# A sum over all rows of h: from VectorE (in layernorm and beside the products of q) to GpSimd, behind each store

## The chip, the cores and the metric

The kernel runs on one core of one Trainium2 chip. The metric is the device time of one execution in microseconds (us). Five engines work side by side and wait for each other by semaphores: TensorE (PE in the profile), VectorE (DVE), ScalarE (ACT), GpSimd (POOL) and SyncE (SP). DMA transfers are issued by SP, ACT and POOL from their own instruction streams; an issue that must wait holds up what is behind it in that stream.

## The reference

x is 2708 × 1024 (f32), adj is 2708 × 2708 with an entry of 1 with probability 0.0014771 (four per row on average), the weights are 1024 × 1024.

```python
h = relu(layernorm(x))
q = h @ W_q.T + b_q;  k = h @ W_k.T + b_k;  v = h @ W_v.T + b_v
z = (q @ k.T) / sqrt(1024)
z = z * adj;  z = where(z == 0, -10000, z)
out = softmax(z, axis=1) @ v
return x + relu(out)
```

For a row with neighbours the masked entries weigh nothing, so only the neighbours' rows are needed. A row without any neighbour has equal weights on all 2708 rows: for it the kernel needs the sum of all rows of h. That sum is what the change is about.

## The kernel before, in words

**The arithmetic.** Scores are h·M·hᵀ with M = W_qᵀ·W_k, formed once on TensorE (`part_of_m`, L348). "q" of a row is then h·M plus a bias row, its score with a neighbour is a dot product with that neighbour's row of h, and the output of a row is (the weighted sum of its neighbours' rows of h) times W_vᵀ. The 2708 rows make 22 tiles of 128 rows (tile 21 has 20).

**Stage 1, layernorm, edges and M** (until about 200 us). `follow` (L235) carries out strings of steps written by hand: `s` = `stats` (L188: load rows of x on SP, VectorE's mean and variance), `r` = `root` (L209: seven small operations, the last is r at L221), `a` = `apply` (L224), `e` = `edges` (L250: load a tile of adj on SP, ACT counts its entries at L256, VectorE finds their places by FIND_INDEX8 at L259 and sorts them into keys). In `apply`, ACT writes relu(layernorm) over the row tile (L230), POOL stores it to h_dram (L231), and, for tiles below EARLY = 9, VectorE adds it to hsum (L233), a 128 × 1024 tile whose column sums are the sum over all rows. Row tiles of x rotate over seven buffers and four more of the tag "q"; adj rotates over three. ACT's order is the written one in this stage, so an eviction of PSUM behind an L230 waits for it. VectorE's, SyncE's and POOL's order is set by a scheduler. Tiles 0 to 4 of q are formed here the plain way (`query`, L309), in natural order of rows.

**The sort.** Rows are sorted by their number of neighbours (`sort`, L467): VectorE makes `hot` (L484) after the last tile's edges, TensorE multiplies it (ps_in at L488, placed within tile 4's product), VectorE works out every row's place (pos_i at L502) and POOL writes the table (`put`, L445). From then on POOL gathers rows of h by the table (L425, L428).

**Stage 2, units.** The units are 8 pairs of tiles of q (5..20; unit numbers n = 0..7), then 10 pairs of output tiles (n = 8..17). Each is a Strassen-like product of seven blocks (`multiply`, L790): TensorE's block products at L780, `blocks` (L513) makes the operands (transposes at L274, sums on VectorE at L524), `q_results` (L821) and `o_results` (L851) take the results (q at L834, p at L859). Up to FIRST = 2 the rows of a pair come in natural order or by `first_rows`; from unit 2 on rows in the sorted order are gathered one unit and more ahead (`load_rows`).

**Attention** is one stream of VectorE steps in tile order 6,5,4,3,0,2,1,9,…: `scores` (L658; L664, 1.22 us a step, on the gathered row g and the query row pq), `weights` (L683; exp on ACT at L680, u on ACT at L709 or, in the two tiles 8 and 20 that hold rows without neighbours, at L703 from hsum) and `sums` (L713; L717, 1.28 us a step). The queries pq come by a gather from q_dram (tiles below 9) or a load from q_late, both on POOL. After each of the seven products `advance(share)` issues attention worth `share` us; an output pair whose rows are not yet done makes it catch up (`advance(1.0)` until done). From unit FIRST on VectorE's order is the written one, so a step of attention stands in front of or behind a product's sums as written.

**hsum before the change.** Tiles below 9 are summed in `apply`. The other rows are added when they have been gathered in sorted order for the pairs of q from unit 2 on: `sum_rows` (L921) adds the two row tiles of the next pair behind its operands' sums (L924, 12 additions), and one gather and addition of the last 20 rows (h_rest) stands in unit 2. `all_rows` (L926) then sums over partitions on TensorE (ps_h) in unit 6, and ACT writes the result back into hsum.

Of the kernel before, what the change touches and what calls it, by code (L numbers as in the profile page):

```python
# [18 lines left out]
P = 128  # L19
# [4 lines left out]
SLOTS = 16  # L24
# [6 lines left out]
EARLY = 9  # L31
# [24 lines left out]
def tile_preln_masked_attention(  # L56
# [12 lines left out]
    nc = tc.nc  # L69
# [6 lines left out]
    FULL = N // P  # L76
    REST = N - FULL * P
# [14 lines left out]
    h_dram = dram.tile([N, D], FT, name="h_dram")  # L92
# [24 lines left out]
    hsum = const.tile([P, D], FT, name="hsum")  # L117
# [36 lines left out]
    t = 0  # L154
    while t < NT:
# [4 lines left out]
        t = e  # L160
# [24 lines left out]
    def row_tile(name):  # L185
        return work.tile([P, D], FT, tag="row", name=name, bufs=ROWS)
# [37 lines left out]
    def apply():  # L224

        group, xs, r = normed.pop(0)
        for i, t in enumerate(group):
            t0, n = tiles[t]
            xt = xs[i]
            nc.scalar.activation(xt[:n], xt[:n], AF.Relu, bias=r[:n, 4, i:i + 1], scale=r[:n, 3, i:i + 1])  # L230
            nc.gpsimd.dma_start(h_dram[t0:t0 + n, :], xt[:n])  # L231
            if t < EARLY:
                nc.vector.tensor_add(hsum[:n], hsum[:n], xt[:n])  # L233

    normed, adj_loads = [], []  # L235

# [56 lines left out]
    def query(hT, banks, name, first=False, between=(), mid=None):  # L293

        q = work.tile([P, D], FT, tag="q", name=f"q_{name}", bufs=4)
        order = [(h, c) for h in range(NH) for c in range(DC)]
        if first:

            order.sort(key=lambda hc: hc[1] >= DC // 2)
        def evict(h):  # L300
            if h < len(between):
                follow(between[h])
            nc.scalar.copy(q[:, h * NB:(h + 1) * NB], banks[h])

        for h, c in order:
            if mid is not None and (h, c) == (1, 3):
                evict(0)
                mid(mm)
            mm = nc.tensor.matmul(banks[h], hT[:, c, :], M[:, c // 4, h, c % 4, :], start=False,  # L309
                                  stop=(c == DC - 1), skip_group_check=True)  # L310
        for h in range(NH) if mid is None else (1,):
            evict(h)
        return q
# [111 lines left out]
    def gather(dst, src, t, w, n, skip=False):  # L425
        off = bass.IndirectOffsetOnAxis(ap=ptab.bitcast(U32)[:n, t, w:w + 1], axis=0)
        if skip:
            return nc.gpsimd.indirect_dma_start(out=dst, out_offset=None, in_=src, in_offset=off,  # L428
                                                bounds_check=N - 1, oob_is_err=False)
        return nc.gpsimd.indirect_dma_start(out=dst, out_offset=None, in_=src, in_offset=off)  # L430

    rows_of = {}
    FIRST = (EARLY - SINGLE) // 2
# [77 lines left out]
    behind = []  # L511

    def blocks(xa, xb):  # L513


        ops = {}

        def held(name, bank):
            ops[name] = small(name).rearrange("p (c q) -> p c q", q=P)
            nc.scalar.copy(ops[name], bank)  # L520

        def put(name, a, b, op):
            ops[name] = small(name).rearrange("p (c q) -> p c q", q=P)
            behind.append(nc.vector.tensor_tensor(ops[name], a, b, op=op))  # L524

        def upper():
            held("a11", half_turned(xa, 0))
            held("a12", half_turned(xa, 1))

        def lower():  # L530
            held("a22", half_turned(xb, 1))
            a21 = half_turned(xb, 0)
            put("s1", ops["a22"], a21, ALU.add)
            put("s3", ops["a11"], a21, ALU.subtract)
            put("s2", ops["s1"], ops["a11"], ALU.subtract)
            put("s4", ops["a12"], ops["s2"], ALU.subtract)

        return ops, upper, lower
# [19 lines left out]
    for t in range(SINGLE):  # L558
# [7 lines left out]
        if t == SINGLE - 1:  # L566
# [3 lines left out]
        q = query(hT.pop(t), banks, f"e{t}", first=(t == 0), between=work_between[t] if t < 4 else (),  # L570
                  mid=sort_here if t == 4 else None)
# [197 lines left out]
    def advance(us):  # L769

        spent[0] -= us
        while spent[0] < 0:
            step = next(stream, None)
            if step is None:
                break
            spent[0] += step
# [5 lines left out]
    def banks_for(row):  # L782

        return_ = []
        for h in range(NH):
            return_.append(psum.tile([P, NB], FT, tag="acc", name=f"ps{h}"))
            nc.scalar.copy(return_[h], row[:, h * NB:(h + 1) * NB])
        return return_
# [91 lines left out]
    def send(keep=0):  # L880
        while len(sent) > keep:
            y, t = sent.pop(0)
            scatter(y, t, P)
# [8 lines left out]
    def of_wv(i, j):  # L892

        return wv[j][:, i * 4:(i + 1) * 4, :]
# [23 lines left out]
    last_q = len(q_pairs) - 1  # L918
    summed = []

    def sum_rows(rows, n=P):  # L921
        with tc.issue_after(behind[-1].ins):
            for row in rows:
                nc.vector.tensor_add(hsum[:n], hsum[:n], row[:n])  # L924

    def all_rows():  # L926

        for h in range(NH):
            ps_h = psum.tile([P, NB], FT, tag="tp", name="ps_h")
            nc.tensor.matmul(ps_h, ones, hsum[:, h * NB:(h + 1) * NB], start=True, stop=True)  # L930
            nc.scalar.copy(hsum[:, h * NB:(h + 1) * NB], ps_h)
        summed.append(True)

    for n, unit in enumerate(units):
        kind, ta, tb = unit
        now[0] = n
        if n == FIRST:
            ordered.enter_context(tc.manual_schedule(engines={mybir.EngineType.DVE}))
        if 1 <= n <= 3:

            i, j = ((0, 0), (1, 0), (1, 1))[n - 1]
            nc.sync.dma_start(m_dram[i, j], M[:, i, j])
        share = (19.0 if kind == "q" else 18.0) / 7
        nxt = units[n + 1] if n + 1 < len(units) else None
        results = (q_results if kind == "q" else o_results)(ta, tb)

        def after(i):
            if i in (2, 5):
                send()
            if n == FIRST - 1 and i == 2:  # L950

                chain.append(behind[-1])
                next(stream)
            if n == FIRST - 1 and i == 6:
                chain.append(behind[-1])
            if n >= FIRST or n == FIRST - 1 and i == 6:
                advance(share)
            if nxt is not None:

                if i == (3 if n == FIRST - 1 else 0):  # L960
                    ops_of[n + 1] = blocks(*rows_of[n + 1])
                    ops_of[n + 1][1]()
                if i == (5 if n == FIRST - 1 else 2):
                    ops_of[n + 1][2]()
                    rows = rows_of.pop(n + 1)
                    if nxt[0] == "q" and n + 1 >= FIRST:
                        sum_rows(rows)
                    if n == last_q - 1:
                        all_rows()
                if i == 3:  # L970
                    banks_of[n + 1] = banks_for(bp_sb)
                if i == 4 and n == FIRST:
                    rest = row_tile("h_rest")
                    gather(rest[:REST], h_dram[:, :], FULL, SLOTS, REST)
                    sum_rows([rest], REST)
                if i == 4 and n + 2 < len(units) and n + 2 not in rows_of:
                    while units[n + 2][0] == "o" and not done.issuperset(units[n + 2][1:]):
                        advance(1.0)
                    rows_of[n + 2] = load_rows(units[n + 2])
            if n == last_q - 1 and i == 4:  # L980

                nc.sync.dma_start(bp_sb, bv.to_broadcast([P, D]))
                nc.vector.tensor_sub(bp_sb[:, NB:], bp_sb[:, NB:], bp_sb[:, :NB])

            for k, at in enumerate(((0, 0), (0, 2), (0, 4), (0, 6), (1, 0), (1, 2), (1, 3))):
                if (n - last_q, i) == at:
                    place, src = ((M[:, 0, 0], of_wv(0, 0)), (T[:, 0], tv_dram[0]), (T[:, 1], tv_dram[1]),
                                  (M[:, 1, 0], of_wv(1, 0)), (T[:, 2], tv_dram[2]), (M[:, 1, 1], of_wv(1, 1)),
                                  (T[:, 3], tv_dram[3]))[k]
                    nc.sync.dma_start(place, src)  # L990

        multiply(ops_of.pop(n)[0], banks_of.pop(n), results, after, None)
# [46 lines left out]
    with tc.If(some > 0):  # L1039
        with tc.tile_pool(name="big", bufs=1, side="right") as big, tc.tile_pool(  # L1040
# [20 lines left out]
            with tc.For_i(0, NT) as i:  # L1061
                r0 = nc.snap(smin(i * P, N - P))
                rows = bass.ds(r0, P)
# [7 lines left out]
                q = gen.tile([P, D + 1], FT, tag="q", name="g_q")  # L1071
# [111 lines left out]
```

## Time and profile before

Three runs took 713.38, 713.4 and 713.5 us, median 713.4. The profile and the trace are of one execution of their own:

| what | value |
|---|---|
| profiled execution | 710.02 us, of which the span of the trace 708.2 |
| granted TensorE clock, mean | 0.995 |
| busy: PE, DVE, ACT, POOL | 676.4, 532.0, 252.1, 301.0 us |
| L233, hsum + x on VectorE | 9 additions, 10.8 us, 1.200 each |
| L924, hsum + qr on VectorE | 12 additions, 14.7 us, 1.227 each |
| L231, store of h on POOL | 22 issues, 0.536 each |
| L664 / L717, steps of attention | 94 of 1.223 / 79 of 1.282 |

A line of the profile gives the engine, the line of the kernel (L12), the operation, its output and inputs by the program's names, how often it ran, and what ended the idle time in front of it. A timeline's line begins with the start and the length in us from the start of the span; several instructions of one kind in succession are one line. The idle time of an engine that is not the bound costs nothing by itself.

### The profile page before, as it was taken

To read this page: it belongs to the slowest core of one execution; us is meant where nothing else is said; L and a number is where in the kernel's file an instruction comes from. 1 tells how busy PE (TensorE), PEld (TensorE's weight loads), DVE (VectorE), ACT (ScalarE), POOL (GpSimd) and SP (SyncE) were. 2 spreads that over 40 slices of the span, in tenths; PEclk is the share of its full clock that TensorE was granted. 3 is DMA by queue.
4 is the path that set the end of the run, shared out by engine and by line. 5 is a ranking of instruction groups with operands and counts; after the bars stand their busy time and mean duration, and the time that the engine had idled before them with its cause. 6 is when DMAs were issued, how large, how long until landed. Compare 5 with 4: busy or idle time off the path is not lost. (4 is left out here: it accounts for less than half of the span.)

```text
span 708.2 us, 6378 instructions
## 1 busy us (share of the span) xinstructions
PE 676.4 (96%) x1812; PEld 346.1 (49%) x1812; DVE 532.0 (75%) x1074; ACT 252.1 (36%) x378; POOL 301.0 (42%) x278
## 2 busy tenths in 40 slices
PE   6999999899999997998999999999999999799995
PEld 4776776444454452444444444444444444344442
DVE  6999848997992039899898898888999996851001
ACT  0077168768721221322322322232423423323220
POOL 2011010000256646867474462786567856231312
PEclk9999999999999999999999999999999999999999
DMA  9999699999996378877789899898789889473524
GB/s 346 406 408 336 269 321 401 409 344 385 393 362 214 121 279 287 296 264 254 266 266 363 313 412 377 238 324 244 226 244 283 271 255 264 118 208 102 138 41 135
DMA packets 62915, 198.02 MB, mean 280 GB/s; under 512 B 9910, under 2 KB 10262, under 8 KB 61468
## 3 DMA queue, kind: packets, MB, share of 16 engines
q0 software_dynamic: 34208, 107.76, 48.1%
q1 hardware_dynamic: 26652, 82.99, 30.8%
q10 hardware_dynamic: 2016, 6.82, 2.5%
q8 instruction: 16, 0.26, 0.1%
q14 instruction: 23, 0.19, 0.1%
HBM read 164.61 MB, written 46.51 MB: 298 GB/s over the span
## 5 line engine op out<-in xcount | busy, mean ns | idle before, releaser
L428 POOL DMA_INDIRECT g<-h_dram,tab x107 | 135.8, 1269 | 50.0 <-issue 22.6
L780 PE MATMUL psy<-T,s 128*128 128x512 f32 x288 | 129.6, 592 | 1.8 <-ACT u L804 1.8
L780 PE MATMUL ps<-M,a 128*128 128x512 f32 x288 | 130.3, 592 | 0.0
L664 DVE SCALAR_TENSOR_TENSOR junk<-g,pq 128x1024 uint8<-128x1024 f32 x94 | 114.9, 1223 | 17.8 <-DMA pq<-q_dram,tab 11.0
L355 PE MATMUL ps_m<-wk,wq 128*128 128x512 f32 x256 | 112.4, 601 | 5.5 <-DMA wq<-in_wq_dram 5.4
L717 DVE SCALAR_TENSOR_TENSOR u<-g,coef,u 128x1024 f32<-128x1024 f32 x79 | 101.3, 1282 | 9.4 <-ACT u L709 7.3
L355 PEld LDWEIGHTS ps_m<-wk,wq 128*128 128x128 f32 x256 | 80.1, 314 | 36.0 <-DMA wk<-in_wk_dram 5.4
L780 PEld LDWEIGHTS psy<-T,s 128*128 128x128 f32 x288 | 54.6, 190 | 70.6 <-issue 65.8
L780 PEld LDWEIGHTS ps<-M,a 128*128 128x128 f32 x288 | 53.4, 190 | 60.7 <-issue 60.5
L231 POOL DMA_DIRECT2D h_dram<-x x22 | 11.8, 536 | 166.9 <-ACT x L230 166.9
L259 DVE FIND_INDEX8 at<-ones,adj 128x8 uint32<-128x685 f32 (+1 forms) x88 | 75.3, 864 | 0.0
L780 PE MATMUL psy<-T,a 128*128 128x512 f32 x144 | 67.1, 610 | 8.4 <-DVE p L859 4.8
L309 PE MATMUL ps<-M,T_e 128*128 128x512 f32 x160 | 69.8, 593 | 1.8 <-ACT ps L290 1.8
L780 PE MATMUL ps<-T,s 128*128 128x512 f32 x144 | 65.4, 593 | 1.8 <-DVE s L524 1.8
L780 PE MATMUL ps<-M,s 128*128 128x512 f32 x144 | 65.2, 592 | 0.0
L256 ACT ACTIVATE sized<-adj 128x2708 uint8<-128x2708 f32 (+1 forms) x22 | 54.1, 2461 | 4.1 <-DMA adj<-in_adj_dram 4.0
L849 POOL DMA_INDIRECT y<-in_x_dram,tab x21 | 34.6, 1645 | 43.4 <-ACT y L864 20.7
L780 PEld LDWEIGHTS psy<-T,a 128*128 128x128 f32 x144 | 27.3, 194 | 44.8 <-issue 30.5
L309 PEld LDWEIGHTS ps<-M,T_e 128*128 128x128 f32 x160 | 30.0, 190 | 37.7 <-issue 35.2
L618 POOL DMA_INDIRECT out_dram<-y,tab x21 | 23.5, 1121 | 49.4 <-DMA y<-in_x_dram,tab 48.5
L780 PEld LDWEIGHTS ps<-M,s 128*128 128x128 f32 x144 | 27.3, 190 | 34.0 <-issue 34.0
L520 ACT COPY a<-pt 128x512 f32<-128x512 f32 x54 | 30.2, 592 | 32.2 <-PE pt L274 22.7
(197 smaller groups left out, 707.8 us busy)
## 6 DMA issues: line engine op xcount, KB each, us to landing
adj<-in_adj_dram SPq DMA_DIRECT2D x21, 1354.0 KB
x<-in_x_dram SPq DMA_DIRECT2D x21, 512.0 KB
h_dram<-x POOLq DMA_DIRECT2D x21, 512.0 KB
q_late<-q SPq DMA_DIRECT2D x12, 512.0 KB
pq<-q_late POOLq DMA_DIRECT2D x12, 512.0 KB
u_dram<-u POOLq DMA_DIRECT2D x9, 512.0 KB
or<-u_dram SPq DMA_DIRECT2D x9, 512.0 KB
wq<-in_wq_dram SPq DMA_DIRECT2D x8, 512.0 KB
```

The lines of the kernel that those rows point to most:

```text
L231: nc.gpsimd.dma_start(h_dram[t0:t0 + n, :], xt[:n])
L256: nc.scalar.activation(sized[:n], a[:n, :, :PW], AF.Abs, accum_out=total[:n, t:t + 1])
L259: nc.vector.max_index(at[:n, g, :], ones[:n, 0:8], a[:n, g, :])
L309: mm = nc.tensor.matmul(banks[h], hT[:, c, :], M[:, c // 4, h, c % 4, :], start=False, stop=(c == DC - 1), skip_group_check=True)
L355: nc.tensor.matmul(acc[i], lhs, wk_sb[o][:, cols], start=(o == 0), stop=(o == DC - 1))
L428: return nc.gpsimd.indirect_dma_start(out=dst, out_offset=None, in_=src, in_offset=off, bounds_check=N - 1, oob_is_err=False)
L520: nc.scalar.copy(ops[name], bank)
L618: to = nc.gpsimd.indirect_dma_start(out=out, out_offset=bass.IndirectOffsetOnAxis(ap=ptab.bitcast(U32)[:n, t, SLOTS:SLOTS + 1], axis=0), i ...
L664: chained(lambda: nc.vector.scalar_tensor_tensor(junk, g_of[t][s], 1.0, tq[t], op0=ALU.mult, op1=ALU.mult, accum_out=zall[:, t, s:s + 1]))
L717: chained(lambda: nc.vector.scalar_tensor_tensor(u, g_of[t][s], coef[:, at[t][s]:at[t][s] + 1], u, op0=ALU.mult, op1=ALU.add))
L780: nc.tensor.matmul(bank, a[:, c, :], b[:, c, :], start=False, stop=(c == 3), skip_group_check=True)
L849: nc.gpsimd.indirect_dma_start(out=y[:n], out_offset=None, in_=x, in_offset=off, compute_op=ALU.add)
```

## The change

Three things are changed. Every tile's addition to hsum in `apply`, for all 22 tiles, is made by GpSimd, on the same queue as the store of that tile and right behind it. The additions of gathered rows in the pairs of q, and the gather and addition of the last 20 rows, are left out. The share of attention issued per pair of products is 20 in the pairs of q and 19 in those of o, in place of 19 and 18.

```diff
@@ apply()
             nc.scalar.activation(xt[:n], xt[:n], AF.Relu, bias=r[:n, 4, i:i + 1], scale=r[:n, 3, i:i + 1])
             nc.gpsimd.dma_start(h_dram[t0:t0 + n, :], xt[:n])
-            if t < EARLY:
-                nc.vector.tensor_add(hsum[:n], hsum[:n], xt[:n])
+            nc.gpsimd.tensor_add(hsum[:n], hsum[:n], xt[:n])
@@ the units
-    def sum_rows(rows, n=P):
-        with tc.issue_after(behind[-1].ins):
-            for row in rows:
-                nc.vector.tensor_add(hsum[:n], hsum[:n], row[:n])
...
-        share = (19.0 if kind == "q" else 18.0) / 7
+        share = (20.0 if kind == "q" else 19.0) / 7
...
                     ops_of[n + 1][2]()
-                    rows = rows_of.pop(n + 1)
-                    if nxt[0] == "q" and n + 1 >= FIRST:
-                        sum_rows(rows)
+                    rows_of.pop(n + 1)
                     if n == last_q - 1:
                         all_rows()
...
-                if i == 4 and n == FIRST:
-                    rest = row_tile("h_rest")
-                    gather(rest[:REST], h_dram[:, :], FULL, SLOTS, REST)
-                    sum_rows([rest], REST)
```

The order of instructions changes with it where the scheduler decides. On POOL each of the 22 additions stands directly behind its store. On SP the load of x's tile 13 stands behind that of tile 11, those of tiles 16 and 17 behind four more loads of adj, the load of h_e7 behind adj 17 to 19 and that of h_e8 behind adj 20 and 21.

## The prediction

> **What bounds the kernel now.** I read the busy shares first, then TensorE's own idle gaps, then what the engines named in those gaps had waited for. Part 1 of the page, and a table by stretch (start and end, length, busy time with instruction count of PE, PEld, DVE, ACT, POOL, then granted clock, DMA share, GB/s):
>
> ```profile
> PE 676.4 (96%) x1812; PEld 346.1 (49%) x1812; DVE 532.0 (75%) x1074; ACT 252.1 (36%) x378; POOL 301.0 (42%) x278
> 100.00:130.00 30.00, 27.11 (x75) 18.50 (x75) 25.51 (x90) 20.93 (x30) 2.14 (x4) 1.00 1.02 390
> 130.00:200.00 70.00, 70.00 (x190) 32.83 (x189) 62.27 (x187) 47.85 (x56) 6.02 (x9) 1.00 1.00 378
> 264.00:325.00 61.00, 53.78 (x143) 24.77 (x142) 55.62 (x88) 14.83 (x26) 43.45 (x36) 0.97 0.84 287
> 325.00:485.00 160.00, 159.79 (x449) 75.83 (x449) 143.00 (x198) 45.45 (x81) 93.08 (x76) 1.00 0.88 309
> 485.00:618.00 133.00, 125.52 (x344) 58.41 (x343) 120.44 (x207) 46.12 (x83) 82.23 (x69) 1.00 0.80 240
> ```
>
> TensorE is the bound. In 130–200 and 325–485 it has no gap, though VectorE is 89% busy in both. So time is to be had only where PE idles: 2.9 us in 100–130, 7.2 in 264–325, 7.5 in 485–618, besides start and end. PE's timeline at those gaps (start, length, idle before it and its releaser in brackets), then ACT's and DVE's:
>
> ```profile
> 112.20 1.09 PE L274 MATMUL pt<-ident,h_e 128*128 128x128 f32 x8 [1.11 <-issue]
> 126.38 4.99 PE L309 MATMUL ps<-M,T_e 128*128 128x512 f32 x11 [1.78 <-ACT ps L290]
> 269.91 3.70 PE L780 MATMUL psy<-T,s 128*128 128x512 f32 x8 [1.83 <-ACT u L804]
> 283.83 5.40 PE L780 MATMUL psy<-T,a 128*128 128x512 f32 x8 [3.35 <-DVE q L834]
> 323.91 1.06 PE L274 MATMUL pt<-ident,qr 128*128 128x128 f32 x8 [2.04 <-DMA qr<-h_dram,tab]
> 611.40 3.70 PE L780 MATMUL psy<-T,a 128*128 128x512 f32 x8 [3.36 <-DVE p L859]
> ```
>
> ```profile
> 106.81 2.37 ACT L230 ACTIVATE x<-x,r 128x1024 f32<-128x1024 f32 x2 [6.29 <-DVE r L221]
> 121.53 2.37 ACT L230 ACTIVATE x<-x,r 128x1024 f32<-128x1024 f32 x2 [1.39 <-DVE r L221]
> ```
>
> ```profile
> 192.95 0.64 DVE L484 TENSOR_TENSOR hot<-deg,down 128x162 f32<-128x162 f32 x2
> 265.38 1.23 DVE L664 SCALAR_TENSOR_TENSOR junk<-g,pq 128x1024 uint8<-128x1024 f32 x1 [10.96 <-DMA pq<-q_dram,tab]
> 278.32 2.51 DVE L924 TENSOR_TENSOR hsum<-hsum,qr 128x1024 f32<-128x1024 f32 x2
> 602.84 1.23 DVE L664 SCALAR_TENSOR_TENSOR junk<-g,pq 128x1024 uint8<-128x1024 f32 x1 [4.80 <-DMA pq<-q_late]
> ```
>
> At 112 and 126 ACT's evictions stand in its written order behind layernorm's L230, which waited for VectorE's r. At 270, 284 and 611 VectorE is late, twice after it had itself waited for a transfer (10.96, 4.80). At 324 a gathered row is late. The product behind the 3.35 gap took 5.40 instead of about 3.6 (granted clock 0.72 in 284–290): 1.8 more lost there.
>
> **The change part by part.** The sum is made against the profiled execution, 710.02 us (span 708.2 and 1.8 around it), 3.4 below the median of 713.4; the difference in us is carried to the median.
>
> *Off VectorE.* Nine L233 adds, 10.8 us by the group's row (1.200 each); twelve L924 adds, 14.7 (1.227 each); one h_rest add, 1.2, with its gather on POOL (the add waited 1.7 for it). Together 26.7 us, but on an engine that costs time only at the gaps. All nine L233 adds lie before about 110; the others in the pairs of q from unit 2 on.
>
> *On to GpSimd.* Twenty-two adds, each right behind its store's issue (L231, 0.536 us), so 21 full and one of 20 rows. No row shows a GpSimd add. Low end: VectorE's own 1.20. High end: three passes of what a GpSimd memset of this size takes (L118, 0.942), 2.8. I take 1.9, two such passes, since two operands must be read: about 41 us, between 26 and 61. POOL is busy 8.2 of the 100 us from 100 to 200, so its time is covered by its own idleness. Behind each add stand the next stores of its group: the last of four comes up to 3 × (0.54 + 1.9 − 1.19) = 3.8 us later, 1.19 being ACT's pace (2.37 for two). Behind the last adds stand the three memsets (187.78, 190.37) and then the puts, which wait 9.42 for pos_i until 200.7: about 10 us of cover. An x row's buffer now comes free after its add too; that hides in the landing of the same row's store, for which the loads wait anyway (15.2 us in three waits on SP), unless the add ends later than it.
>
> [...]
>
> *Queues.* SyncE's order changes: x_13 now directly behind x_11; the loads of h_e7 and h_e8 behind adj tiles 17–19 and 20–21. Before, h_e8's load waited 161.5 to 171.6 for a store and kept the last two adj loads behind it until 172.06; x_15's waited for x_8's store until 98.09 and kept adj loads back. So r at 106.8 can come sooner (in front of it VectorE waited 2.49 for x at 103.08), and the last adj tiles, too. What they feed is the sort: VectorE waits for adj 19 until 174.95, is then busy without a break until hot at 193.59, and PE's ps_in, which needs hot, starts at 194.70. Slack: about 1 us.
>
> *100–130.* Both gaps, 1.11 and 1.78, can go, 2.9 us at most. But PE then reaches ps_in 2.9 earlier, and hot has 1 us of slack and perhaps 1.3 from adj 19 (h_e7's half megabyte at the 390 GB/s of the first row no longer ahead of it). The gain is thus bounded by 2.3, and I take 1.5. Low side: the last tiles' GpSimd adds run beside the sort chain. Small DVE operations of two inputs there (cand and r, 0.14–0.19 each, some fourteen from 175 to 191) are few; if half waited half an add (0.95), hot would be 6.7 later, and PE loses 5.7 beyond the slack. No row of before shows such interference, so I take none and keep −2.3 to +5.7.
>
> [...]
>
> *Pairs of q.* Share rises from 19 to 20 per pair in seven products: 20/1.27 ≈ 15.7 steps of attention in place of 15.0. VectorE's bill per pair falls by 2.45 and rises by about 1 (25 to 23.4), against 25.8 for seven products and the transposes: under the bound before and after. In unit 2 the pair of L924 adds at 278.32 (2.51) stands right before the late q (283.09, 0.68) that ends the 3.35 gap. It goes; one more attention step (1.27) comes in front. VectorE's q would come 1.24 earlier. But TensorE's written order now holds 0.86 us less of other work ahead of that wait, so PE gains 0.4. The waits of 1.83 and 2.04 end on transfers and stay: qr's gather takes 7.2 us behind others on POOL. Best case: all of 1.83 + 3.35 and the slow product's 1.8, 7.0. Worst: the shorter cover costs where nothing was late; unit 5's transposes are demanded before 6 us of products that were ahead of them; I bound it by one gap of 2. I take −0.4, range −5 to +2 (the best case needs every one of them).
>
> *Pairs of o.* Share 18 to 19. Attention done by then is more: from p22 of unit 10 to that of unit 14 I count 70 steps where 73 stood, 3.8 us less for VectorE. Against it PE has 3.45 us less of hoisted work in front of unit 14's wait (the 3.36 gap), and VectorE's 4.80 wait for pq<-q_late lies on the way and does not depend on adds: that load is issued by POOL behind gathers. Nearly equal, so 0; range −4 to +3.5 (a gap longer by 1.7 and a slowed product of 1.8 behind it, as at 284).
>
> [...]
>
> Sum: −1.5 − 0.4 + 0 = −1.9. 708.1 for the profiled execution, 711.5 for the median.
>
> **The rivals.**
> A (forecast, small gain): 711.5, own range 709.5 to 712.
> B (no change): r stays tied to x's landing (2.49 of DMA wait in front of it, DMA share 1.02), what little is won is given back at ps_in, and the removed VectorE time was hidden. Speaks for it: 160 us without a gap at 89% DVE. 713.4.
> C (large gain): the VectorE waits at 270, 284 and 611 all go with the slowed product, on top of A: 1.83 + 3.35 + 1.8 on q, or about 3 to 4 on o. Against: two of three follow from transfers. 704 to 709.
> D (slower): GpSimd's adds of the last tiles hold VectorE up on its way to hot at L484, where PE has 1 us of slack plus what was gained at 112 and 126 counted against it. It decides once VectorE loses over 1 us from 175 to 193; half of the bound, 3.3 on hot, gives +2.3: 715.7, and the full bound 719.
> E (slower): the o pairs' long wait grows, since less work is hoisted in front of it: +2 to +3.5, 715.5 to 717.
> That the adds do not move, or that the stores wait for them, is excluded by the order of POOL's instructions: each add stands directly behind its own store.
>
> **How the numbers follow.** 0.2% is about 1.4 us, and that is what a measurement of this kernel can tell from no change. Chances: A 0.32, B 0.20, C 0.15, D 0.20, E 0.13. A lies partly inside 0.2% (above 712.0): I give 0.28 of it to faster. Faster: 0.28 + 0.15 = 0.43. Same: B and the rest of A, and the mild edge of D and E (0.03): 0.27. Slower: 0.30. The likeliest is A, 711.5. For the range I leave out the far end of C (below 706.5, 0.07) and of D and E (above 717, 0.08): 706.5 to 717.
>
> **What would show it.** Right: 22 adds of 1.2 to 2.8 us on POOL; the gaps at 112 and 126 gone or under 1 us; ps_in 1 to 2 earlier; gap in unit 2 near 3; PE's whole idle time 2 us shorter. Wrong: DVE's cand or r operations, or FIND_INDEX8 (0.87), longer while POOL adds; a PE gap in front of ps_in; a new gap of over 3 us in units 5 or 14 with slow products behind it; adds far over 2.8, so that stores or x loads come late.

## The result: no change

The changed kernel took 714.14 us (median of 12 runs, 711.16 to 717.74), the kernel before 713.97 (12 runs of the same sessions, 712.61 to 715.83). The ratio is 1.0001, 95% interval 0.9981 to 1.0021. Ratios here and below are those on record, and they can differ by some tenths of a per cent from the quotient of the two medians beside them. Below, 1% is counted as 7.1 us. The profiled execution has a span of 710.6 us (before: 708.2); single executions of one kernel lie up to 1.5% apart here (709.22 and 719.55 in one session of the kernel before), so traces are read for their places and mechanisms, and worths are taken from the ratios.

The page's first part and the table by stretch (start and end, length, busy time of PE, PEld, DVE, ACT, POOL with counts, granted clock, DMA share, GB/s) of the changed kernel:

```profile
PE 679.8 (96%) x1812; PEld 348.0 (49%) x1812; DVE 520.8 (73%) x1052; ACT 252.5 (36%) x378; POOL 348.3 (49%) x301
100.00:130.00 30.00, 26.69 (x72) 18.81 (x71) 25.08 (x78) 21.25 (x28) 14.20 (x10) 0.96 1.01 387
130.00:200.00 70.00, 70.00 (x188) 32.87 (x187) 66.68 (x196) 49.01 (x58) 20.23 (x16) 0.99 0.99 365
264.00:325.00 61.00, 54.47 (x147) 25.15 (x146) 53.77 (x89) 17.14 (x29) 46.56 (x40) 0.97 0.87 304
325.00:485.00 160.00, 160.00 (x452) 76.52 (x451) 137.89 (x193) 44.19 (x78) 89.98 (x76) 1.00 0.89 314
485.00:618.00 133.00, 126.15 (x341) 58.87 (x340) 118.32 (x207) 47.76 (x83) 80.02 (x68) 0.97 0.83 247
```

VectorE was relieved of 26.7 us of additions, but it is only 11.2 us less busy (532.0 to 520.8). In 130–200 it is even busier than before (66.7 against 62.3), with nearly the same work. TensorE's idle gaps (timeline of PE; start, length, idle before it and its releaser):

```profile
127.56 15.69 PE L308 MATMUL ps<-M,T_e 128*128 128x512 f32 x32 [3.31 <-ACT ps L289]
273.39 5.40 PE L779 MATMUL psy<-T,s 128*128 128x512 f32 x8 [2.45 <-ACT u L803]
286.22 3.70 PE L779 MATMUL psy<-T,a 128*128 128x512 f32 x8 [1.42 <-DVE q L833]
293.43 1.06 PE L273 MATMUL pt<-ident,qr 128*128 128x128 f32 x8 [2.65 <-DMA qr<-h_dram,tab]
608.11 5.74 PE L779 MATMUL psy<-T,a 128*128 128x512 f32 x8 [4.97 <-DVE p L858]
```

Of the two layernorm gaps of before (1.11 and 1.78) the first went, and the second grew to 3.31. The matrix work behind it took 15.69 in place of 14.00 (granted clock 0.96 in that stretch). The line of before:

```profile
126.38 14.00 PE L309 MATMUL ps<-M,T_e 128*128 128x512 f32 x32 [1.78 <-ACT ps L290]
```

In the pairs of q the gap that ends on VectorE's q fell from 3.35 to 1.42, and the one on ACT's u in front of it grew from 1.83 to 2.45; the slowed product of 5.40 (granted clock 0.72 in 273–279) now stands behind the gap on u. The wait for a gathered row at 324 is gone, and another one, of 2.65, came at 293. In the pairs of o the small gaps shrank, and the long one grew from 3.36 to 4.97 with a slowed product (5.74, granted clock 0.65 in 608–614) behind it.

Where VectorE's time went is seen in the groups of instructions between 55 and 200 us, before and after (busy time, mean ns of one, idle time before):

```profile
L261 DVE TENSOR_TENSOR cand<-first,at 128x32 f32<-128x32 f32 x19 | 3.4, 180 | 0.2
L262 DVE SCALAR_TENSOR_TENSOR cand<-at,cand 128x32 f32<-128x32 uint32 x19 | 3.4, 180 | 0.2
```

```profile
L260 DVE TENSOR_TENSOR cand<-first,at 128x32 f32<-128x32 f32 x18 | 9.8, 546 | 0.3
L261 DVE SCALAR_TENSOR_TENSOR cand<-at,cand 128x32 f32<-128x32 uint32 x19 | 8.1, 428 | 0.3
L232 POOL TENSOR_TENSOR hsum<-hsum,x 128x1024 f32<-128x1024 f32 x21 | 49.6, 2362 | 0.4
```

The two cand operations of `edges`, 32 columns wide, take 0.18 us alone and up to 2.8 beside an addition of GpSimd (2.36 each). Two of them in VectorE's timeline, and the additions beside them in GpSimd's:

```profile
111.95 1.08 DVE L260 TENSOR_TENSOR cand<-first,at 128x32 f32<-128x32 f32 x1
127.91 2.21 DVE L261 SCALAR_TENSOR_TENSOR cand<-at,cand 128x32 f32<-128x32 uint32 x1
```

```profile
110.61 2.36 POOL L232 TENSOR_TENSOR hsum<-hsum,x 128x1024 f32<-128x1024 f32 x1
127.70 2.35 POOL L232 TENSOR_TENSOR hsum<-hsum,x 128x1024 f32<-128x1024 f32 x1
```

111.95 + 1.08 = 113.03 and 110.61 + 2.36 = 112.97: VectorE's operation ends 0.06 us after GpSimd's. The second pair does the same (130.12 and 130.05). Of the 44 cand operations nine met an addition, and each of the nine ended 0.05 to 0.07 us after it. FIND_INDEX8, with 0.866 us against 0.865, and the layernorm's statistics, 0.669 against 0.670, are not touched. Over the whole layernorm the 44 cand operations took 20.5 us in place of 7.9: 12.6 us, more than the 10.8 of the nine additions that VectorE was rid of there.

### The profile page after: what moved, and what is told of

Its sections match the earlier page's. It is cut to its first block, busy times and chain, and to the rows that moved or that the text cites. A ratio compares the mean times of both kernels' runs of the same rounds, so it can differ in the third digit from the quotient of the medians.

```text
span 710.6 us, 6380 instructions
## 1 busy us (share of the span) xinstructions
PE 679.8 (96%) x1812; PEld 348.0 (49%) x1812; DVE 520.8 (73%) x1052; ACT 252.5 (36%) x378; POOL 348.3 (49%) x301
## 5 line engine op out<-in xcount | busy, mean ns | idle before, releaser
L427 POOL DMA_INDIRECT g<-h_dram,tab x107 | 128.7, 1203 | 41.9 <-issue 24.0
L779 PE MATMUL psy<-T,s 128*128 128x512 f32 x288 | 131.3, 599 | 2.5 <-ACT u L803 2.5
L308 PE MATMUL ps<-M,T_e 128*128 128x512 f32 x160 | 71.4, 604 | 3.3 <-ACT ps L289 3.3
L232 POOL TENSOR_TENSOR hsum<-hsum,x 128x1024 f32<-128x1024 f32 (+1 forms) x22 | 52.0, 2363 | 0.5
L617 POOL DMA_INDIRECT out_dram<-y,tab x21 | 24.8, 1181 | 40.9 <-DMA y<-in_x_dram,tab 39.7
```

What stands on the lines that cost most here:

```text
L232: nc.gpsimd.tensor_add(hsum[:n], hsum[:n], xt[:n])
L617: to = nc.gpsimd.indirect_dma_start(out=out, out_offset=bass.IndirectOffsetOnAxis(ap=ptab.bitcast(U32)[:n, t, SLOTS:SLOTS + 1], axis=0), i ...
L779: nc.tensor.matmul(bank, a[:, c, :], b[:, c, :], start=False, stop=(c == 3), skip_group_check=True)
```

## The experiments

Four theories. **1**: a GpSimd addition holds up VectorE's operations of two SBUF inputs until it ends, and that ate the gain. **2**: VectorE's time was hidden, so nothing could be won. **3**: the stretch comes from something other than an addition's length. **4**: the higher share costs what the additions won. All ratios are against the kernel before on the same chip, with 95% intervals.

### Additions cut in four

```diff
-            nc.gpsimd.tensor_add(hsum[:n], hsum[:n], xt[:n])
+            for k in range(0, D, D // 4):
+                nc.gpsimd.tensor_add(hsum[:n, k:k + D // 4], hsum[:n, k:k + D // 4], xt[:n, k:k + D // 4])
```

> The changed kernel, with each GpSimd addition cut into four of 256 columns; every engine's order of instructions is otherwise that of the changed kernel. Theory 1 (a GpSimd addition blocks a VectorE operation of two SBUF inputs until it ends, and that ate the gain in layernorm): the two cand operations (0.546 and 0.428 us mean with the additions whole, 0.180 without) fall to 0.22 to 0.32, since one can wait for a quarter of 0.6 us only; TensorE's gap near 127 is 2.3 to 3.0 in place of 3.3 and no slowed product follows it; 712 to 713.5. Theory 2 (the removed VectorE time was hidden, the stretched operations are hidden too): the operations may shrink, the time stays 713.5 to 714.5. Theory 3 (the stretch is not from the additions' length): operations stay at 0.43 and over.

714.51 against 715.09; 1.001 (0.9985 to 1.0035). VectorE's timeline and GpSimd's at one of the places:

```profile
156.46 2.20 DVE L261 TENSOR_TENSOR cand<-first,at 128x32 f32<-128x32 f32 x1
158.69 0.65 DVE L262 SCALAR_TENSOR_TENSOR cand<-at,cand 128x32 f32<-128x32 uint32 x1
```

```profile
156.51 2.77 POOL L233 TENSOR_TENSOR hsum<-hsum,x 128x256 f32<-128x256 f32 x4
```

Four quarters take 2.77 together. The first cand operation waits through three of them, not through one, and the second through the last. All cand operations together took 22.8 us: 16 of them are stretched now in place of nine, five by more than one quarter (0.72), the others by less. So the block was not one instruction long here: three quarters in a row kept VectorE out for 2.20 us. Cutting them bought nothing (1.001); the expectation of theory 1 was wrong in that detail.

### A copy in place of the addition

```diff
-            nc.gpsimd.tensor_add(hsum[:n], hsum[:n], xt[:n])
+            nc.gpsimd.tensor_copy(hsum[:n], xt[:n])
```

The sum over rows is left out here, as in all the runs below without additions.

> The changed kernel, with each GpSimd addition replaced by a copy of x into hsum (one SBUF input; the sum over rows is left out, so rows without neighbours come out wrong). Order of instructions as in the changed kernel. Theory 1 with a block by any GpSimd read of SBUF: copies of 1.0 to 1.4 us, cand at 0.25 to 0.4 us, time 712.5 to 714. Theory 1 with a block only by two inputs on both sides: cand at 0.18, time 711.5 to 713. Theory 2: 713.5 to 714.5 whatever cand does.

711.07 against 715.09; 0.9955 (0.9923 to 0.9987). The groups from 55 (VectorE) and from 40 (GpSimd) to 200:

```profile
L261 DVE SCALAR_TENSOR_TENSOR cand<-at,cand 128x32 f32<-128x32 uint32 x19 | 4.8, 250 | 0.3
L260 DVE TENSOR_TENSOR cand<-first,at 128x32 f32<-128x32 f32 x18 | 3.9, 215 | 0.3
```

```profile
L232 POOL COPY hsum<-x 128x1024 f32<-128x1024 f32 x21 | 22.1, 1052 | 0.0
```

Every engine has the order of the changed kernel, GpSimd is busy 29 us less, and the cand operations are stretched by 2.0 us in all (9.9 against 7.9). Both together are worth some 0.46%, 3.3 us, over the changed kernel, with some 2.7 us of uncertainty either way. Two cand operations were stretched by a copy:

```profile
61.93 0.76 DVE L260 TENSOR_TENSOR cand<-first,at 128x32 f32<-128x32 f32 x1
62.73 1.47 DVE L261 SCALAR_TENSOR_TENSOR cand<-at,cand 128x32 f32<-128x32 uint32 x1
```

```profile
61.59 1.05 POOL L232 COPY hsum<-x 128x1024 f32<-128x1024 f32 x1
63.09 1.05 POOL L232 COPY hsum<-x 128x1024 f32<-128x1024 f32 x1
```

They end at 62.69 and 64.20, the copies at 62.64 and 64.14. So these copies, with one SBUF input, held VectorE's operation up until 0.05 and 0.06 us after their end, as the additions did; they are only shorter (1.05 against 2.36) and met fewer of the operations.

### No additions at all

```diff
-            nc.gpsimd.tensor_add(hsum[:n], hsum[:n], xt[:n])
```

> The changed kernel without the additions (the sum over rows is left out, so rows without neighbours come out wrong): 26.7 us less for VectorE than before, nothing more for GpSimd. Theory 1: cand back at 0.18 us, TensorE's gaps near 112 and 127 under 2.5 together, 710.5 to 712.5. Theory 2: VectorE's time is hidden and the gaps end on transfers, 713 to 714.5.

707.66 against 715.09; 0.9906 (0.9875 to 0.9936), 6.7 us faster than before and more than either theory had. The cand operations are at 7.95 in all. Layernorm has no gap left on TensorE; the work that waited 3.31 in the changed kernel stands directly behind its forerunner, and the next gaps are those of the pairs of q:

```profile
122.82 1.04 PE L272 MATMUL pt<-ident,h_e 128*128 128x128 f32 x8
123.69 13.90 PE L307 MATMUL ps<-M,T_e 128*128 128x512 f32 x32
265.83 3.70 PE L778 MATMUL psy<-T,s 128*128 128x512 f32 x8 [0.55 <-ACT u L802]
278.66 3.70 PE L778 MATMUL psy<-T,a 128*128 128x512 f32 x8 [3.12 <-DVE q L832]
285.79 1.06 PE L272 MATMUL pt<-ident,qr 128*128 128x128 f32 x8 [2.57 <-DMA qr<-h_dram,tab]
```

SyncE's order is partly another one here (x tiles 8 to 11 are loaded in front of an adj tile), which the scheduler chose. So the 6.8 us between this run and the changed kernel hold that order besides the additions; the run with copies has the changed kernel's order.

### The old share, and the square of both parts

Additions on GpSimd, shares of 19 and 18:

> The changed kernel with the old shares of 19 and 18: the additions moved, and no more attention per product. Theory 1: shares matter little, 713.5 to 714.5. Theory 4 (the higher share of attention costs what the removed additions win, by the wait of 4.97 us near 608 and the slowed product behind it): that gap under 4, 711.5 to 713.

725.08 against 715.09; 1.0154 (1.0118 to 1.019). Neither theory had this: with the old share the change would have cost 11 us. TensorE's timeline:

```profile
284.53 5.40 PE L779 MATMUL psy<-T,a 128*128 128x512 f32 x8 [3.50 <-DVE q L833]
294.66 1.50 PE L273 MATMUL pt<-ident,qr 128*128 128x128 f32 x8 [2.16 <-DMA qr<-h_dram,tab]
326.41 1.94 PE L273 MATMUL pt<-ident,qr 128*128 128x128 f32 x8 [4.09 <-issue]
```

The transposes of pair 5 now stand earlier in TensorE's order, as the prediction said. The profile names no releaser for the 4.09, but the rows were gathered late: POOL issued the gather of qr at 318.38, behind gathers of g that wait for VectorE to give a slot back, and VectorE stood idle 3.02 and 1.68 us at 302 and 305, waiting for ACT's u and a with no attention issued to it in between. With the new share the same gather was issued at 313.73 and TensorE had no gap there. So the share does not only use VectorE, it also moves the queue of gathers. This gap is only part of the 11 us, and it does not follow from the share alone: at the old share it is 2.04 before and 2.14 without additions (below), and the kernel before has one of 2.57 there at the new share.

The kernel before with the new shares:

> The kernel before with the new shares of 20 and 19, its additions all left on VectorE. With the changed kernel (ratio 1.000), the additions moved and old shares (1.015) it makes the square of both parts. If the parts simply add up, the share is worth 1.5% here too: about 0.985, 704. If the share only brings VectorE work that the removed additions leave room for, VectorE has no room here: 713 to 718.

717.41 against 714.95; 1.0037 (1.0005 to 1.0068). This fits the second case of the expectation, that VectorE has no room here. The long gap of the pairs of o is 6.79, but it doesn't show that by itself, since the run without additions, 6.7 us faster than before, has 5.93 there:

```profile
615.60 5.25 PE L780 MATMUL psy<-T,a 128*128 128x512 f32 x8 [6.79 <-DVE p L859]
```

No additions and the old shares:

> No additions anywhere (the sum over rows is left out) and the old shares of 19 and 18; TensorE's order as in the run with the additions moved and old shares, which took 725. If GpSimd's additions cost the 6.5 us that leaving them out won at the new shares: 717 to 720, slower than before, and so VectorE's relief without more attention per product is worth less than nothing. If the slowdown of that run came from GpSimd's additions: 708 to 712.

712.92 against 714.95; 0.9989 (0.996 to 1.0019). So the square is:

| additions | shares 19, 18 | shares 20, 19 |
|---|---|---|
| on VectorE, as before | 1 | 1.0037 |
| on GpSimd | 1.0154 | 1.0001 |
| none | 0.9989 | 0.9906 |

Relieving VectorE alone is worth next to nothing (0.9989, with no change inside its interval). With the relief, the higher share is worth 0.9906 / 0.9989, 0.8% or 5.9 us; without it, it costs 0.4%. GpSimd's additions, with the order of loads that came with them, cost 1.0001 / 0.9906, 1.0% or 6.8 us, at the new share, and 1.7% at the old one. The change is the sum: −0.8 − 5.9 + 6.8 = +0.1 us. By the intervals each of these three terms is uncertain by some 2 to 3 us.

### The same additions in the same place, on VectorE

```diff
-            nc.gpsimd.tensor_add(hsum[:n], hsum[:n], xt[:n])
+            nc.vector.tensor_add(hsum[:n], hsum[:n], xt[:n])
```

> The changed kernel with the same 22 additions in the same place, on VectorE: 26 us of VectorE in layernorm, nothing on GpSimd. Theory 1 (a GpSimd addition blocks VectorE): 26 us of additions against the 12 us by which they stretched VectorE's operations; the last ones lie on the way to hot and make TensorE wait in front of ps_in, 2 to 6: 713 to 719. If GpSimd's place behind the store (buffers, stores, memsets) was what cost: 708 to 711.

717.2 against 714.95; 1.0038 (1.0016 to 1.0059). As theory 1 had it: the cand operations are unstretched (7.7 us in all), but hot ends at 201.3 (before 193.6; 1.2 us of that stand ahead of the first ps_v product, see the table below), ACT's evictions behind layernorm's steps are late again, and TensorE waits twice about three us:

```profile
127.91 15.42 PE L308 MATMUL ps<-M,T_e 128*128 128x512 f32 x32 [3.18 <-ACT ps L289]
190.97 11.40 PE L308 MATMUL ps<-M,T_e 128*128 128x512 f32 x22 [2.94 <-ACT ps L289]
```

So 26 us of additions on VectorE cost 0.4% more than GpSimd's 52 us and the 12.6 that these put on VectorE.

### More share still

> The changed kernel with shares of 21 and 20. If attention further ahead keeps shortening the waits for gathered rows: 709 to 712. If VectorE is late for TensorE's operands and results once it carries more (24.4 us of a pair's 25.8): 715 to 720.

Shares of 21 and 20: 713.14 against 714.95; 0.9977 (0.9953 to 1.0002). At best a little; the change of sign is not settled.

### Additions held until VectorE has done its operation of two inputs

Tiles 12 to 19 wait for a cand operation; tiles 20 and 21 go to VectorE behind pos_i:

```diff
+        masked = nc.vector.scalar_tensor_tensor(cand[:n], at[:n], float(PW) - 0.5, cand[:n], op0=ALU.is_lt,
+                                                op1=ALU.mult)
+        while unsummed and t < NT - 2:
+            xt, m = unsummed.pop(0)
+            behind_cand = nc.gpsimd.tensor_add(hsum[:m], hsum[:m], xt[:m])
+            tc.add_manual_dep(behind_cand.ins, masked.ins.name, ...)
...
         placed = nc.vector.tensor_copy(pos_i, deg)
+        with tc.issue_after(placed.ins):
+            while unsummed:
+                xt, m = unsummed.pop(0)
+                nc.vector.tensor_add(hsum[:m], hsum[:m], xt[:m])
```

> The changed kernel, with the GpSimd additions of tiles 12 to 19 held by a semaphore until VectorE has finished the second cand operation of the next adj tile (so that they run beside FIND_INDEX8, which has one input), and the additions of tiles 20 and 21 on VectorE behind pos_i. TensorE's and SyncE's order as in the changed kernel. Theory 1 (what the additions cost is VectorE's two-input operations waiting beside them, in 107 to 190): cand from 100 to 190 at 0.18 to 0.25 us, TensorE's gap near 127 below 2 and no slowed product behind it, hot 2 us earlier or more; 709 to 712. Rival (the additions cost by GpSimd's own lateness, by buffers or by DMA, or by the stretches before 72): 713 to 715.

718.85 against 715.61; 1.0031 (1.0003 to 1.006): slower, against the expectation. Layernorm did as expected in part (gap near 127 of 2.75, cand operations behind 100 us stretched by 3.5 in place of 6.7), but a new gap came in the first pairs of q, with a slowed product. TensorE, GpSimd and VectorE there:

```profile
255.00 6.35 PE L793 MATMUL psy<-T,a 128*128 128x512 f32 x8 [3.67 <-DVE q L847]
```

```profile
206.68 0.97 POOL L458 DMA_INDIRECT tab_dram<-tab,pos_i  x1 [0.30 <-issue]
207.95 7.99 POOL L458 DMA_INDIRECT tab_dram<-tab,pos_i  x1 [0.30 <-issue]
216.25 1.14 POOL L458 DMA_INDIRECT tab_dram<-tab,pos_i  x1 [0.30 <-issue]
```

```profile
213.22 1.27 DVE L618 TENSOR_TENSOR g<-g 128x512 f32<-128x512 f32 x2
214.42 0.67 DVE L615 TENSOR_TENSOR g<-g 128x512 f32<-128x512 f32 x1
215.13 0.69 DVE L616 TENSOR_TENSOR g<-g,g 128x512 f32<-128x512 f32 x1
215.85 0.69 DVE L617 TENSOR_TENSOR g<-g,g 128x512 f32<-128x512 f32 x1
```

One of the puts of the table, the fourth, took 7.99 us, in the changed kernel 1.38. VectorE ran operations of two inputs without a gap from 202.5 to 215.1; the put ended with the next small gaps at 215.1 and 215.8. The table was then late (VectorE's first use of it at 253.6 against 250.2), and VectorE's q, which stands behind that use, made TensorE wait. The same with shares of 21 and 20:

> As e9_gated, with shares of 21 and 20. If both gains add (21 and 20 were worth 0.2 to 0.3% on the changed kernel): 707.5 to 710.5, below both kernels. If the higher share only helped to make up for what the blocked operations lost: as e9_gated.

718.99 against 715.61; 1.0054 (1.0023 to 1.0085), with the same put of 7.99 and a gap of 3.39 at the same place. The share helped nothing.

### Three additions from the rows that the first pairs load

As above for tiles 12 to 19, but tiles 20 and 21 again on GpSimd behind their stores, and tiles 5 to 7 added by VectorE from the natural rows of pairs 0 and 1, behind the run of subtractions:

```diff
+            if t < 5 or 8 <= t < 12 or t >= 20:
+                nc.gpsimd.tensor_add(hsum[:n], hsum[:n], xt[:n])
+            elif t >= 12:
+                unsummed.append((xt, n))
...
-                    rows_of.pop(n + 1)
+                    rows = rows_of.pop(n + 1)
+                    if n == 0:
+                        with tc.issue_after(behind[-1].ins):
+                            for row in rows_of.pop(0) + rows[:1]:
+                                nc.vector.tensor_add(hsum, hsum, row)
```

> The changed kernel with the stretched operations avoided in another way: tiles 5 to 7 are added by VectorE from the rows of h that pairs 0 and 1 have loaded (in its idle time near 220, behind the rows of T and W_v), tiles 12 to 19 on GpSimd behind a cand operation, the others as in the changed kernel. TensorE, ACT and SyncE in the order of the changed kernel, VectorE with three additions more. If the stretches at 62 to 71 (4.6 us) and from 107 on are the cost and the loss of the last two kernels came from the two additions behind pos_i: cand stretched by under 4 us in all, r of tiles 8 to 11 (89.3) 2 to 4 earlier, ps_in (197.2) 2 to 4 earlier, no gap at 255; 709 to 712. If GpSimd's additions cost by something else: 713 to 716.

711.58 against 715.95; 0.9955 (0.9926 to 0.9985): faster than the kernel before, and by the ratios than the changed one. TensorE and VectorE:

```profile
125.41 14.00 PE L318 MATMUL ps<-M,T_e 128*128 128x512 f32 x32 [2.29 <-ACT ps L299]
```

```profile
216.26 3.74 DVE L973 TENSOR_TENSOR hsum<-hsum,h_e 128x1024 f32<-128x1024 f32 x3
```

r of tiles 8 to 11 came at 86.8 (89.3 in the changed kernel) and ps_in at 194.7 (197.2). But 1.4 us of each stand ahead of the first ps_v product; measured from there both came only 1.1 earlier, under the 2 to 4 that were expected. Nothing waits at 255, and no put up to 215 took over 1.50. The cand operations are still stretched by 8.1 us in all, so the expectation of under 4 was missed: a held pair of additions, 4.8 us, runs into the next tile's cand.

### The additions of tiles 4 to 7 left out

> The changed kernel with the additions of tiles 4 to 7 left out (their rows are missing from the sum, so rows without neighbours come out wrong); SyncE's early order is then again that of the kernel without additions (x loads in front of an adj load). If the early stage, before 72, is where most of the 6.8 us went that the additions cost: 709 to 711. If the later stretches carry it: 712 to 714.5.

711.59 against 715.95; 0.9945 (0.9918 to 0.9971). This does not place the cost: with SyncE's early order changed, the remaining additions met other cand operations, and these took 22.7 us in all, more than with all additions. r of tiles 8 to 11 was 4.0 us earlier measured from the first ps_v product, ps_in only 0.6. That the time fell all the same shows that the sum of the stretches does not by itself set it.

### Marks of layernorm in these kernels

TensorE reaches its first ps_v product at 61.7 to 63.5 us, and two runs with the same layernorm (before, and before with the new shares) already differ there by 1.2. So marks behind it are compared from that product on. In us behind it: the r of tiles 8 to 11, the r in front of TensorE's wait near 127, and the start of ps_in:

| kernel | ps_v | r, 8 to 11 | r near 127 | ps_in |
|---|---|---|---|---|
| before; with the new shares | 62.1; 63.3 | 25.9; 26.4 | 59.3; 59.3 | 132.3; 132.9 |
| changed; old share; shares 21, 20 | 63.5; 62.0; 62.0 | 25.8; 25.9; 26.6 | 59.0; 60.5; 60.1 | 133.7; 135.2; 134.8 |
| copies | 62.4 | 24.3 | 56.9 | 131.4 |
| no additions; at the old share | 63.1; 62.8 | 21.1; 20.6 | 52.0; 51.5 | 128.5; 128.5 |
| without those of 4 to 7 | 61.9 | 21.8 | 55.2 | 133.1 |
| three from the rows of the first pairs | 62.1 | 24.8 | 58.3 | 132.6 |

At the new share the additions on GpSimd put ps_in off by 5.3 us, where they cost 6.8 in all; at the old one by 6.8. Two causes are mixed in this. The three runs with SyncE's other order have r of tiles 8 to 11 at 20.6 to 21.8, even the one whose remaining additions stretch more than all of them did; the copies, with little stretch and the changed kernel's order, have it at 24.3. So some 3 us there come from the order of loads and not from the waiting operations. From the changed kernel to the copies ps_in gains 2.3 us in the same order. How much of the 6.8 us the waiting alone costs was not tested: only the copies take it away in the same order, and they shorten GpSimd's own time as well.

## Why the prediction was right and wrong

The range (706.5 to 717) held the result, and the sum's likeliest, a small gain to 711.5, did not come; the time is that of rival B, no change, but for B's reason only in half. That it lies so near the forecast is luck: the gain of the relief with the higher share and the cost of GpSimd's additions are each near 6.8 us, the sum had the one at 1.9 and the other at nothing, and they cancelled. Step by step:

- *Off VectorE, "costs time only at the gaps".* Right: at the old share the additions left out are worth 0.8 us of their 26.7, no change within the interval. B's sentence that the removed time was hidden is right for this part.
- *On to GpSimd, 1.9 us each, covered by its own idleness.* Measured 2.36, inside the bounds of 1.20 and 2.8. At the end it was covered (GpSimd waits 10.22 us for pos_i), and SyncE waited only 0.5 us in all for an addition; no run separates what GpSimd's own time cost from the rest.
- *"No row of before shows such interference, so I take none and keep −2.3 to +5.7."* This is the step that failed. VectorE's cand operations did wait for GpSimd's additions, 12.6 us in all, and GpSimd's additions cost 6.8 us at the new share. With copies in the same order, which stretch by 2.0, 3.3 of them are won back; the rest is the copies' own time, their stretch and the order of loads together. The bound of 5.7 was of the right size, but it was derived for the sort chain alone (175 to 191), where after shows one stretch of 0.9; most of it came before, at 53 to 72, 112, 128, 156 and 173. In front of TensorE's wait near 127 the additions took back all that the relief had won for VectorE's r: measured from the first ps_v product it came at 59.0 as before (59.3), at 56.9 with copies, and at 52.0 without additions and in SyncE's other order. The gap there was 0.4 longer than the two it replaced, and the slowed work behind it added 1.7. The nine cand operations that met an addition ended 0.05 to 0.07 us behind it, and FIND_INDEX8 (0.866 against 0.865) was not touched. Giving such waits no weight at all, for want of a row, was the error: a change that puts a new kind of work beside another can't have a row of before.
- *100–130, gain of 1.5, at most 2.3.* Without GpSimd's additions, and with the order of loads that came with that, the gain was there and larger: from the first ps_v product to ps_in it was 132.3 us before, 133.7 in the changed kernel and 128.5 without additions. So 3.8 us were to be won and 1.4 were lost. That hot would bind at 1 us of slack was wrong, since by the same measure hot came 5.9 us earlier as well. (The 194.70 from which that slack was read is the second ps_in product; the first starts at 194.37, so it was 0.8.)
- *Pairs of q, −0.4 and share as a small item on VectorE's bill.* The gap in unit 2 went from 3.35 to 1.42, but this is no pure gain: the wait for u just in front of it grew with its product, and without additions, where that wait is 0.55, the gap is 3.12. Both waits together went from 5.18 to 3.87, 1.3 us and not 0.4. And the sum had no term for what more attention ahead is worth over the whole kernel: 5.9 us with room on VectorE. That this goes by POOL's queue of gathers is read from the trace of one run and not tested alone.
- *Pairs of o, 0, range −4 to +3.5.* Rival E's mechanism came true in the trace, 4.97 with a slowed product in place of 3.36, about +3.6 at that place; smaller gaps that went took 2.2 of it back.

Shown by the runs: the block, and the worth of the parts in the square. Not shown: how the 6.8 us divide between the waiting operations, SyncE's order and GpSimd's own time, or among the single stretches, since every kernel that moved them moved something else too; and by which way the share gains. The median of before lies 4 to 6 us above its profiled execution, that of the changed kernel 2 above its own; what of the worths lies in clock dips that the one trace of before has few of (mean granted clock 0.995, in the other executions of before 0.982 to 0.998) stays open as well.

## What to carry to other kernels

Moving the additions from VectorE to GpSimd was not free here: VectorE's small operations of two SBUF inputs beside them (cand, 0.18 us alone) took up to 2.83, to the end of the addition, and 2.20 through three quarters in a row where the additions were cut. For a like move, look for such operations in VectorE's stream at the place it goes to, and weigh in the sum that each may wait like this. Compare orders too: leaving work out can change what a scheduler does elsewhere, here the loads of x. Free time on VectorE was worth something here only with a setting that filled it: with the sum left out, the relief gave 0.8 us and the relief with a higher share 6.7; the share without relief was a loss. Where several parts of a change act on each other, test them in a square and not one by one.

## What the runs showed of the hardware

- A GpSimd addition of 128 × 1024 with two SBUF inputs took 2.36 us, a quarter of it 0.72, a copy 1.05; the one of 20 rows took as long (2.39).
- VectorE operations of 32 columns with two SBUF inputs ended 0.05 to 0.07 us after the GpSimd addition beside them (nine of nine), and 0.05 and 0.06 after a copy with one SBUF input; cutting the addition in four back to back let one of them wait 2.20 us still. FIND_INDEX8 took 0.866 in the kernel with additions on GpSimd and 0.865 in the one before.
- The other way round, an indirect DMA issue of GpSimd took 7.99 us, in two kernels, beside an unbroken run of VectorE operations of two SBUF inputs. The changed kernel has such a run at 203 to 215 with issues of at most 1.5, so what makes the difference is open.
- Gaps on TensorE of 2.45, 2.75 and 3.31 were followed by slowed products (5.40 in place of 3.6 to 3.7, 15.70 and 15.69 in place of 14.00), others of 3.12 and 3.27 were not (3.70, 14.00), and one of 3.12 in the run with copies was (5.40): their length alone did not decide it.
